# A graph attention block on one core: half of VectorE's evictions listed one step later, behind the score maximum, and the output projection's blocks and sums in another order

## The chip, the cores and the metric

The kernel runs on one core of one Trainium2 chip. The metric is the device time of one execution in microseconds (us). A core has five engines that each work through a list of their own, in the order in which the program gives it: TensorE (PE; its weight loads are PEld in the profile), VectorE (DVE), ScalarE (ACT), GpSimd (POOL), and SyncE (SP), which here issues most of the DMAs. Engines wait for each other at semaphores.

## The reference

The input x has 384 rows (nodes) of 1024 features. With h = relu(layernorm(x)), the block computes

```
q  = h @ wq.T + bq      k  = h @ wk.T + bk      v  = h @ wv.T + bv
q2 = q @ wiq.T + biq    k2 = k @ wik.T + bik    v2 = v @ wiv.T + biv     (16 heads of 64)
scores = q2 @ k2.T / 8 + mask        (per head, 384 x 384; the mask is built from 6528 edges)
out    = x + softmax(scores) @ v2 @ wo.T + bo
```

All seven weights are 1024x1024 in float32.

## The kernel before

**Precision.** Most products are made of three matmuls in a rounded float32: every operand is split into a "hi" part and a "lo" part (lo = value - hi), and the helper `mm3` (lines 373 to 376) issues hi*hi, hi*lo and lo*hi. So whatever leaves PSUM and is multiplied again is evicted twice: ScalarE writes hi, then VectorE (sometimes GpSimd) subtracts and writes lo. The same holds for each 128x1024 slice of a weight: `load` brings it into `raw` over SP's queue (4 buffers), `split_hi` rounds it on ScalarE (L81) or VectorE (L79), `split_lo` writes the rest on VectorE or GpSimd (L86).

**Stages.** First layernorm; then the projections v, q, iv and k with the mask built beside them (up to some 145 us); then a stage in which three things run woven together: the second projections of q and k for eight pairs of heads (generator `fill_qk`), the attention of 48 tiles (16 heads times 3 row tiles), and, when `fill_qk` has run out, the output projection (generator `fill_o`). This last stage is where the change lies.

**The steps of the last stage.** The loop `for i in range(S + 11)` with S = 48 writes the order of all engines' lists by hand; one turn of it is called a step here. `manual_schedule` keeps that order. A step lists, in this order: half of its share of generator work on PE (`fill(r / 2)`), the two score matmuls of tile i (`do_S`, L711), the other half of the share; then `do_ttr(i - 1)` (L717 on VectorE: it reads the scores from PSUM, adds the mask and takes the row's maximum; called ttr below), `do_low` (L748, VectorE), `do_exp(i - 2)` (ScalarE), `do_norm(i - 3)` (L734 and L736 on VectorE, L738 on GpSimd), `do_high` (L744, ScalarE); then PE's transposes of two earlier tiles woven with the product of another head with v2 (`turns_and_av`, L758 and L773); then the evictions of what was transposed one step ago (`do_pt`: hi on ScalarE in L766, lo on VectorE in L767) and of the product of one step ago (`do_ao`: ScalarE L793, VectorE L794), the splitting of a finished pair of heads (`do_aos`: ScalarE L798, GpSimd L799), and the tasks that the generators left (`run_tasks`: `qk_done`, which evicts a finished q or k projection in L384 and L385 and copies it into stacks over SP's queue, and `qk_head`, which splits the weight slice w + 2 and loads the slice w + 5). One tile in three is transposed by a DMA (`do_turn`, L752 on SP) in place of PE. In the steps of `WSTEPS` a slice of wo is prepared by `wo_prep` (split, and the load of the slice three further on).

**The output projection.** The result is six blocks (three row tiles times two halves of 512 columns); block a is `OT[a]`. Each sums eight slices of wo, one per pair of heads: `omm(t, h, k)` adds slice k with one `mm3`. The first four slices (k < KH = 4) make a first half that `ysum` (L663, VectorE) adds into the residual; the other four start a new sum in PSUM. The PSUM banks called "g" are three, and also serve the q and k projections. So a fourth block can start only when the `ysum` of the first has read its bank. `ysums` holds the blocks whose first half is complete; `flush_y(n)` lists the sums of the first n of them. Before, `fill_o` itself calls it, at the moment when a new block asks for its bank:

```
            if k == 0:
                flush_y(1)
                oacc[OT[a]] = bank("g")
            omm(*OT[a], k)
            if k == KH - 1:
                ysums.append(a)
```

**PSUM.** Scores have two banks ("s"), transposes two ("t"), the product with v2 one ("a"), all others three ("g"). From step 49 on, when the scores are done, two of the output's blocks take "s" banks (`bank_step`).

Of the kernel before, what the change touches and what calls it, by code (L numbers as in the profile page):

```python
# [13 lines left out]
PSC = 32768.0  # L14
AF = mybir.ActivationFunctionType
OP = mybir.AluOpType
AX = mybir.AxisListType

N, D, NT, KT, NP = 384, 1024, 3, 8, 8
# [7 lines left out]
def gnn_kernel(ctx: ExitStack, tc: tile.TileContext, x, edges, erows, etw, wq, wk, wv, wiq, wik, wiv, wo,  # L27
# [6 lines left out]
    nc = tc.nc  # L34
# [13 lines left out]
    def bank(tag):  # L48
        return psum.tile([128, 512], F32, tag=tag, name=tag, bufs={"g": 3, "a": 1}.get(tag, 2))

    def gtile(tag):
        return big.tile([128, 2, KT, N], F32R, tag=tag, name=tag)
# [11 lines left out]
    def load(w):  # L64
        if w >= NCH:
            return
        n, m = chunks[w]
        raw[w] = wpool.tile([128, D], F32, tag="raw", name="raw", bufs=4)
        nc.sync.dma_start(raw[w], W[n][m])

    def split_hi(w, dst=None, dve=False):
        if w >= NCH:
            return
        if dst is None:
            t = wpool.tile([128, 2, D], F32R, tag="whl", name="whl", bufs=4)
            dst = (t[:, 0, :], t[:, 1, :])
        whl[w] = dst
        if dve:
            nc.vector.tensor_copy(dst[0], raw[w])  # L79
        else:  # L80
            nc.scalar.activation(dst[0], raw[w], AF.Copy)  # L81

    def split_lo(w, eng=None):
        if w < NCH:
            hi, lo = whl[w]
            (eng or nc.vector).tensor_tensor(lo, raw[w], hi.bitcast(F32), OP.subtract)  # L86

    def split(w, lo_eng=None, dst=None, hi_dve=False):
        split_hi(w, dst, hi_dve)
        split_lo(w, lo_eng)  # L90
# [151 lines left out]
    def mask_select(g):  # L242

        nc.vector.copy_predicated(ma, mbt[g].bitcast(I32), mbt[g])
# [148 lines left out]
    w = 0  # L393
# [109 lines left out]
    top, up, down = vsc[:, 0:1], vsc[:, 1:2], vsc[:, 2:3]  # L503
    accs = [bank("ststag"[i]) for i in range(6)]
    for k in range(8):
        slot_head(w)
        hi, lo = whl[w]
# [82 lines left out]
                    (q2 if r else nc.sync).dma_start(kf[r * 64:(r + 1) * 64, o, :, :], nf[o * 64:(o + 1) * 64, :, :])  # L590
            stacks["k", p] = ks

    tasks = []

    def run_tasks():
        while tasks:
            tasks.pop(0)()

    def qk_head(w):
        if pendq:  # L600
            pendq.pop(0)()
        if 0 < w - W0 < NTAB:
            mask_select(w - W0)
        split_hi(w + 2)
        split_lo(w + 2, nc.gpsimd if (w + 2) % 2 == PAR else None)
        load(w + 5)
        if w == W0:
            mask_select(0)
# [19 lines left out]
    WO = NCH - 8  # L628

    DT = (0,)  # L630
    PRE, RATE, RATE_O, RATE_E = 84, 7.9, 8, 8
    WSTEPS = (37, 40, 42, 44, 47, 51)
    PAR, OPOOL, ODVE = 1, (2, 3, 4, 6), (2,)

    otile = {}
# [1 line left out]
    KH = 4  # L637

    def wo_prep(k):

        dst = None
        if k == 4:
            otile[0] = gtile("g3").rearrange("p a k n -> p (a k n)")
        if 4 <= k < 7:
            g, b = otile[0], (k - 4) * 2048
            dst = (g[:, b:b + 1024], g[:, b + 1024:b + 2048])
        split(WO + k, nc.gpsimd if k in OPOOL else None, dst, k in ODVE)
        load(WO + k + 3)

    def omm(t, h, k, c=(0, 512)):  # L650
        hi, lo = (a[:, h * 512 + c[0]:h * 512 + c[1]] for a in whl[WO + k])
        mm3(oacc[t, h][:, c[0]:c[1]], ao[:, 0, k, t * 128:(t + 1) * 128], ao[:, 1, k, t * 128:(t + 1) * 128],
            hi, lo, k in (0, KH), k in (KH - 1, KT - 1))
# [3 lines left out]
    now = [-1]  # L657
    wready = [0, 0] + [99] * 6

    def ysum(a, c=(0, 512)):  # L660
        t, h = OT[a]
        y = xb[t][:, h * 512 + c[0]:h * 512 + c[1]]
        nc.vector.tensor_tensor(y, oacc[t, h][:, c[0]:c[1]], y, OP.add)  # L663
        return y
# [3 lines left out]
    def flush_y(n=6):  # L668
        for _ in range(min(n, len(ysums))):
            ysum(ysums.pop(0))  # L670

    def fill_o():


        first = [(0, 0), (0, 1), (1, 0), (1, 1), (2, 0), (2, 1)]
        first += [(a, k) for k in (2, 3) for a in range(3)] + [(a, k) for a in range(3, 6) for k in range(KH)]
        for a, k in first:
            while now[0] < wready[k] or now[0] < 6 * k + OREADY:
                yield 0
            if k == 0:  # L680
                flush_y(1)
                oacc[OT[a]] = bank("g")
            omm(*OT[a], k)
            if k == KH - 1:
                ysums.append(a)
            yield 4
        bank_step = (0, 0, 0, 49, 50)
        todo = [(a, k) for k in range(KH, 7) for a in range(5)]
        while todo:
            ready = [q for q in todo if now[0] >= max(6 * q[1] + OREADY, wready[q[1]], bank_step[q[0]])]  # L690
            if not ready:
                yield 0
                continue
            a, k = ready[0]
            todo.remove(ready[0])
            if k == KH:
                flush_y(1)
                oacc[OT[a]] = bank("gggss"[a])
            omm(*OT[a], k)
            yield 4  # L700

    st_ps, es, sts, tps, avs, aof = {}, {}, {}, {}, {}, {}
    S = 48

    def do_S(i):
        h, t = divmod(i, 3)
        p, o = divmod(h, 2)
        qs, ks = stacks["q", p], stacks["k", p]
        ps = st_ps[i] = bank("s")
        for s in range(2):  # L710
            nc.tensor.matmul(ps[:, :N], qs[:, o, t * 128:(t + 1) * 128], ks[:, o, s, :], start=(s == 0), stop=(s == 1))  # L711

    def do_ttr(i):
        t = i % 3
        e = es[i] = work.tile([128, N], F32, tag="e", name="e", bufs=EB)
        s = sts[i] = work.tile([128, 4], F32, tag="s", name="s", bufs=12)
        nc.vector.tensor_tensor_reduce(e, st_ps.pop(i)[:, :N], ma[:, t, :], -0.125, 3.0e38, OP.add, OP.min, s[:, 0:1])  # L717
# [43 lines left out]
    def do_pt(i):  # L761
        h, t = divmod(i, 3)
        pt = ptv[h % 3]
        hi, lo = (pt[:, s * 3:s * 3 + 3, t * 128:(t + 1) * 128] for s in range(2))
        pv = tps.pop(i)[:, :N].rearrange("p (k n) -> p k n", k=3)
        nc.scalar.activation(hi, pv, AF.Copy, scale=PSC)  # L766
        nc.vector.scalar_tensor_tensor(lo, pv, PSC, hi, op0=OP.mult, op1=OP.subtract)  # L767

    def av_mm(h):
        ps = avs[h] = bank("a")  # L770
# [15 lines left out]
    def do_ao(h):  # L786
        p, o = divmod(h, 2)
        if o == 0:
            aof[p] = work.tile([128, N], F32, tag="aof", name="aof")
        tmp = work.tile([128, N], F32, tag="aot", name="aot", bufs=1)  # L790
        ps = avs.pop(h)
        m, l = slice(o * 64, o * 64 + 64), slice(64 - o * 64, 128 - o * 64)
        nc.scalar.activation(tmp[m, :], ps[l, :N], AF.Identity, scale=down[l], bias=bc[m, 40 + p:41 + p])  # L793
        nc.vector.scalar_tensor_tensor(aof[p][m, :], ps[m, :N], down[m], tmp[m, :], op0=OP.mult, op1=OP.add)  # L794

    def do_aos(h):
        p = h // 2
        nc.scalar.activation(ao[:, 0, p, :], aof[p], AF.Copy)  # L798
        nc.gpsimd.tensor_tensor(ao[:, 1, p, :], aof[p], ao[:, 0, p, :].bitcast(F32), OP.subtract)  # L799
# [4 lines left out]
    def fill(n):  # L804
        credit[0] += n
        while credit[0] > 0 and gens:
            try:
                c = next(gens[0])
            except StopIteration:
                gens.pop(0)  # L810
                continue
            if c == 0:
                credit[0] = 0.0
                return
            credit[0] -= c
# [4 lines left out]
    t_at, a_at = {}, {}  # L820
    for h in range(16):
        for t in (1, 2):
            t_at.setdefault(3 * h + 7 if h < 15 else 3 * h + 5 + t, []).append(3 * h + t)
        a_at[3 * h + 10 if h < 15 else 3 * h + 9] = h
    for i in range(S + 11):
        now[0] = i
        r = RATE if len(gens) == 2 else RATE_O if i < S else RATE_E
        fill(r / 2)
        if i < S:
            do_S(i)  # L830
        fill(r / 2)
        if 0 <= i - 1 < S:
            do_ttr(i - 1)
        if 0 <= i - 4 < S and (i - 4) % 3 in DT:
            do_low(i - 4)
        if 0 <= i - 2 < S:
            do_exp(i - 2)
        if 0 <= i - 3 < S:
            do_norm(i - 3)
            if (i - 3) % 3 in DT:  # L840
                do_high(i - 3)
        turns_and_av(t_at.get(i, []), [a_at[i]] if i in a_at else [])
        for x in t_at.get(i - 1, []):
            do_pt(x)
        if i - 1 in a_at:
            do_ao(a_at[i - 1])
        if a_at.get(i - 2, 0) % 2:
            do_aos(a_at[i - 2])
        run_tasks()
        if 0 <= i - 4 < S and (i - 4) % 3 in DT:  # L850
            do_turn(i - 4)
        if i in WSTEPS:
            wo_prep(wp)
            wready[wp] = i + 2
            wp += 1
    while gens:
        now[0] = 999
        fill(999)
# [55 lines left out]
```

## Time and profile before

| | |
|---|---|
| median of 3 runs | 296.02 us (294.78, 296.02, 296.08) |
| the profiled execution | 294.56 us, of which the span from first to last instruction is 292.8 us |
| granted TensorE clock | 1.000 over the span |
| PE busy | 284.7 us (97%), 1610 instructions |
| VectorE busy | 208.2 us (71%), 509 instructions |
| ScalarE busy | 159.7 us (55%), 291 instructions |
| GpSimd busy | 154.8 us (53%), 153 instructions |
| VectorE from 160 us to 250 us | between 6.65 and 8.16 us busy in each 10 us |
| VectorE from 260 us to 270 us | 8.41 us busy of 10 |

How to read it: busy time is the time that an engine's instructions occupy it; matmuls are pipelined, so a PE that is busy all the time can still be fed unevenly. "Idle before, releaser" of an instruction is how long its engine stood still before it and which event of another engine ended that. Buffers are named without their numbers: "g" is a PSUM bank of the three or a large SBUF tile of the same name, "whl" a split weight slice, "s" a bank of scores or the small tile of row sums, "res" the residual. Positions in time are us from the span's start.

### The profile page before, as it was taken

The numbers are of one execution on the slowest core, as the hardware profiler recorded it, in microseconds if no ns is written. First come the engines' busy times: TensorE is split into PE (matmuls) and PEld (weight loads), VectorE is DVE, ScalarE is ACT, GpSimd is POOL, SyncE is SP. The second block draws the span as 40 slices with busy tenths as digits, with TensorE's granted clock in tenths as the row PEclk, the third lists the DMA queues.
The fourth block names the chain that finished last, engine by engine and source line by source line (L and its number), as shares of the span: only waits on it lengthen the run. The fifth ranks groups of instructions, "written<-read, shape, count | busy, mean of one in ns | idle before, by whom it ended". The sixth has DMA issues, their size and how long they took to land. (4 is left out here: it accounts for less than half of the span.)

```text
span 292.8 us, 4859 instructions
## 1 busy us (share of the span) xinstructions
PE 284.7 (97%) x1610; PEld 267.4 (91%) x1610; DVE 208.2 (71%) x509; ACT 159.7 (55%) x291; POOL 154.8 (53%) x153
## 2 busy tenths in 40 slices
PE   6999999999999999999999999999999999989995
PEld 5999999999988889999999999999999998868874
DVE  3858996667665452999966768878786876788623
ACT  3894543244331222343643778787878788766510
POOL 3765576437775787992004256262627268636210
PEclk9999999999999999999999999999999999999999
DMA  7799857973463342278438879879797969901105
GB/s 268 248 321 404 292 209 254 323 242 112 143 189 122 121 146 72 72 224 296 154 86 227 241 208 211 212 166 227 166 234 147 254 133 234 230 2 27 27 3 215
DMA packets 33305, 54.60 MB, mean 187 GB/s; under 512 B 17408, under 2 KB 20992, under 8 KB 33280
## 3 DMA queue, kind: packets, MB, share of 16 engines
q1 hardware_dynamic: 30896, 51.90, 61.4%
q0 software_dynamic: 2064, 1.80, 2.2%
q10 hardware_dynamic: 320, 0.59, 0.8%
q8 instruction: 13, 0.21, 0.3%
q14 instruction: 12, 0.10, 0.1%
HBM read 38.30 MB, written 3.39 MB: 142 GB/s over the span
## 5 line engine op out<-in xcount | busy, mean ns | idle before, releaser
L374 PE MATMUL g<-g,whl 128*128 128x384 f32 x312 | 105.8, 339 | 0.0
L376 PE MATMUL g<-g,whl 128*128 128x384 f32 x312 | 104.3, 334 | 0.0
L375 PE MATMUL g<-g,whl 128*128 128x384 f32 x312 | 104.2, 334 | 0.0
L231 POOL DMA_INDIRECT tab<-val,idx x51 | 59.7, 1171 | 32.0 <-issue 11.8
L81 ACT ACTIVATE whl<-raw 128x1024 fp32r<-128x1024 f32 x51 | 53.5, 1050 | 29.8 <-PE g L376 21.1
L86 DVE TENSOR_TENSOR whl<-raw,whl 128x1024 fp32r<-128x1024 f32 x41 | 53.8, 1313 | 20.1 <-ACT whl L81 17.0
L374 PEld LDWEIGHTS g<-g,whl 128*128 128x128 f32 x312 | 58.6, 188 | 0.2
L375 PEld LDWEIGHTS g<-g,whl 128*128 128x128 f32 x312 | 58.6, 188 | 0.0
L376 PEld LDWEIGHTS g<-g,whl 128*128 128x128 f32 x312 | 58.6, 188 | 0.1
L390 ACT ACTIVATE g<-f,bc 128x384 fp32r<-128x384 f32 x24 | 14.8, 618 | 53.7 <-DVE f L389 44.8
L738 POOL TENSOR_TENSOR e<-e,s 128x384 f32<-128x384 f32 x32 | 26.4, 829 | 31.2 <-DVE s L734 23.0
L86 POOL TENSOR_TENSOR whl<-raw,whl 128x1024 fp32r<-128x1024 f32 x11 | 26.3, 2395 | 25.9 <-ACT whl L81 25.0
L721 ACT ACTIVATE e<-e,s 128x384 f32<-128x384 f32 x48 | 29.1, 607 | 2.0 <-DVE s L717 1.2
L717 DVE CUSTOM_DVE_ANT_0 e<-s,ma 128x384 f32<-128x384 f32 x48 | 26.4, 552 | 4.3 <-PE s L711 3.7
L389 DVE TENSOR_TENSOR f<-g,rrow 128x384 f32<-128x384 f32 x24 | 13.3, 554 | 18.0 <-PE g L376 18.0
L773 PE MATMUL a<-pt,vhl 128*128 128x384 f16 x96 | 26.1, 326 | 0.0
L758 PE MATMUL t<-ident,e 128*128 128x128 f32 x96 | 24.9, 272 | 0.0
L711 PE MATMUL s<-ks,qs 128*128 128x384 f32 x96 | 24.5, 335 | 0.0
L767 DVE SCALAR_TENSOR_TENSOR pt<-t,pt 128x384 f16<-128x384 f32 x32 | 16.6, 549 | 8.2 <-ACT pt L766 8.2
L799 POOL TENSOR_TENSOR g<-aof,g 128x384 fp32r<-128x384 f32 x8 | 8.3, 1041 | 25.5 <-ACT g L798 25.5
L711 PEld LDWEIGHTS s<-ks,qs 128*128 128x128 f32 x96 | 17.5, 188 | 0.9
L744 ACT ACTIVATE pt<-e,s 128x384 f16<-128x384 f32 x16 | 9.9, 616 | 15.4 <-issue 9.4
(166 smaller groups left out, 447.0 us busy)
## 6 DMA issues: line engine op xcount, KB each, us to landing
ks<-nat SPq DMA_DIRECT2D x30, 192.0 KB
raw<-in_wv_dram SPq DMA_DIRECT2D x8, 512.0 KB
raw<-in_wq_dram SPq DMA_DIRECT2D x8, 512.0 KB
raw<-in_wiv_dram SPq DMA_DIRECT2D x8, 512.0 KB
raw<-in_wk_dram SPq DMA_DIRECT2D x8, 512.0 KB
raw<-in_wiq_dram SPq DMA_DIRECT2D x8, 512.0 KB
raw<-in_wik_dram SPq DMA_DIRECT2D x8, 512.0 KB
raw<-in_wo_dram SPq DMA_DIRECT2D x8, 512.0 KB
```

What stands on the lines that cost most here:

```text
L81: nc.scalar.activation(dst[0], raw[w], AF.Copy)
L86: (eng or nc.vector).tensor_tensor(lo, raw[w], hi.bitcast(F32), OP.subtract)
L231: nc.gpsimd.indirect_dma_start(out=tabs[c // RNG], out_offset=bass.IndirectOffsetOnAxis(ap=idx[:, c:c + 1], axis=0), in_=val[:, c:c + 1], ...
L374: nc.tensor.matmul(ps, lhi, rhi, start=first, stop=False)
L375: nc.tensor.matmul(ps, lhi, rlo, start=False, stop=False)
L376: nc.tensor.matmul(ps, llo, rhi, start=False, stop=last)
L711: nc.tensor.matmul(ps[:, :N], qs[:, o, t * 128:(t + 1) * 128], ks[:, o, s, :], start=(s == 0), stop=(s == 1))
L717: nc.vector.tensor_tensor_reduce(e, st_ps.pop(i)[:, :N], ma[:, t, :], -0.125, 3.0e38, OP.add, OP.min, s[:, 0:1])
L721: nc.scalar.activation(es[i], es[i], AF.Exp, bias=s[:, 0:1], scale=-1.0, accum_out=s[:, 1:2])
L738: nc.gpsimd.tensor_tensor(es[i], es[i], s[:, 2:3].to_broadcast([128, N]), OP.mult)
L758: nc.tensor.transpose(ps[:, k * 128:(k + 1) * 128], es[i][:, k * 128:(k + 1) * 128], ident)
L773: nc.tensor.matmul(ps[:, :N], vhl[:, k, h, :, :], ptv[h % 3][:, 3 * s + k, :], start=(k == 0 and s == 0), stop=(k == 2 and s == 1))
```

## The change

Four things are changed in the last stage.

1. A list `later` is added, and `run_later()`, called in each step just behind `do_ttr`. Four kinds of VectorE instructions are put there in place of being listed at once, so that they stand one step later, behind the next step's ttr: the lo of a weight slice (`split_lo` in `qk_head` and `wo_prep`, where VectorE does it), the lo of transposed tiles (`do_pt`), and the second half of `do_ao`. `do_aos`, which reads the result of `do_ao`, moves from step i - 2 to i - 3 of its head, and the loop has one step more.
2. `fill_o` no longer calls `flush_y`; `flush_y()` stands at the end of every step, and lists the sums of all blocks completed by then.
3. The order of the output's `mm3`: the first three blocks now go by pairs of slices (block 0 with slices 0 and 1, block 1, block 2, then each with 2 and 3), where before slice 2 went over the three blocks and then slice 3. In the second half block 2, which takes a "g" bank, comes behind blocks 3 and 4.
4. `WSTEPS` begins with 36 and 38 in place of 37 and 40, so that slices 2 and 3 of wo are prepared one and two steps sooner, with the loads that these calls issue.

```diff
-    tasks = []
+    tasks, later = [], []
+
+    def run_later():
+        for f in later[:]:
+            f()
+        later.clear()
...
         split_hi(w + 2)
-        split_lo(w + 2, nc.gpsimd if (w + 2) % 2 == PAR else None)
+        eng = nc.gpsimd if (w + 2) % 2 == PAR else None
+        if eng is None and now[0] >= 0:
+            later.append(lambda: split_lo(w + 2))
+        else:
+            split_lo(w + 2, eng)
         load(w + 5)
...
-    WSTEPS = (37, 40, 42, 44, 47, 51)
+    WSTEPS = (36, 38, 42, 44, 47, 51)
     PAR, OPOOL, ODVE = 1, (2, 3, 4, 6), (2,)
...
-        split(WO + k, nc.gpsimd if k in OPOOL else None, dst, k in ODVE)
+        split_hi(WO + k, dst, k in ODVE)
+        if k in OPOOL:
+            split_lo(WO + k, nc.gpsimd)
+        else:
+            later.append(lambda: split_lo(WO + k))
         load(WO + k + 3)
...
-        first = [(0, 0), (0, 1), (1, 0), (1, 1), (2, 0), (2, 1)]
-        first += [(a, k) for k in (2, 3) for a in range(3)] + [(a, k) for a in range(3, 6) for k in range(KH)]
+        first = [(a, k) for c in (0, 2) for a in range(3) for k in (c, c + 1)]
+        first += [(a, k) for a in range(3, 6) for k in range(KH)]
...
             if k == 0:
-                flush_y(1)
                 oacc[OT[a]] = bank("g")
...
-        todo = [(a, k) for k in range(KH, 7) for a in range(5)]
+        todo = [(a, k) for k in range(KH, 7) for a in (0, 1, 3, 4, 2)]
...
             if k == KH:
-                flush_y(1)
                 oacc[OT[a]] = bank("gggss"[a])
...
-        nc.vector.scalar_tensor_tensor(lo, pv, PSC, hi, op0=OP.mult, op1=OP.subtract)
+        later.append(lambda: nc.vector.scalar_tensor_tensor(lo, pv, PSC, hi, op0=OP.mult, op1=OP.subtract))
...
-        nc.vector.scalar_tensor_tensor(aof[p][m, :], ps[m, :N], down[m], tmp[m, :], op0=OP.mult, op1=OP.add)
+        dst = aof[p][m, :]
+        later.append(lambda: nc.vector.scalar_tensor_tensor(dst, ps[m, :N], down[m], tmp[m, :], op0=OP.mult, op1=OP.add))
...
-    for i in range(S + 11):
+    for i in range(S + 12):
...
             do_ttr(i - 1)
+        run_later()
...
-        if a_at.get(i - 2, 0) % 2:
-            do_aos(a_at[i - 2])
+        if a_at.get(i - 3, 0) % 2:
+            do_aos(a_at[i - 3])
...
             wp += 1
+        flush_y()
     while gens:
```

## The prediction

> **What bounds the kernel now.** I read the page first.
>
> ```profile
> PE 284.7 (97%) x1610; PEld 267.4 (91%) x1610; DVE 208.2 (71%) x509; ACT 159.7 (55%) x291; POOL 154.8 (53%) x153
> ...
> PEclk9999999999999999999999999999999999999999
> ```
>
> TensorE is busy for 284.7 of 292.8 us at full clock, so at most 8.1 us can be won by feeding it better, and the change adds and removes no matmul. The second view is who PE waits for, over the whole span:
>
> ```profile
> PE s L295 <- ACT g L283: 1.5, 1, 1.5
> PE g L315 <- POOL ident masks.py:199: 1.4, 1, 1.4
> PE g L374 <- DVE res L663: 1.4, 1, 1.4
> PE g L295 <- DVE g L287: 0.4, 1, 0.4
> ```
>
> Three of the four lie in the first 10 us, which the diff does not touch. The third is the only wait in the last stage: a block of the output projection asks for its bank and the `ysum` of an earlier block (L663) has not read it yet. The rest of the 8.1 us is the start and the 3.3 us between the last matmul and the last output byte. The third view is the timeline at that place, VectorE and then PE:
>
> ```profile
> 256.49 0.56 DVE L767 SCALAR_TENSOR_TENSOR pt<-t,pt 128x384 f16<-128x384 f32 x1 [0.26 <-ACT pt L766]
> 257.18 0.62 DVE L794 SCALAR_TENSOR_TENSOR aof<-a,vsc,aot 64x384 f32<-64x384 f32 x1
> 258.27 1.23 DVE L86 TENSOR_TENSOR g<-raw,g 128x1024 fp32r<-128x1024 f32 x1 [0.46 <-ACT g L81]
> 259.51 0.69 DVE L663 TENSOR_TENSOR res<-g,res 128x512 f32<-128x512 f32 x1
> ```
>
> ```profile
> 258.37 0.51 PE L711 MATMUL s<-ks,qs 128*128 128x384 f32 x2
> 260.25 0.50 PE L374 MATMUL g<-whl,g 128*128 128x512 f32 x1 [1.37 <-DVE res L663]
> 260.59 0.40 PE L375 MATMUL g<-whl,g 128*128 128x512 f32 x1
> ```
>
> Block 1 had its last matmul of slice 3 at 252.3, but its sum was listed only when block 4 asked for the bank, behind the evictions of step 44 and the 1.23 us lo of a wo slice, which itself waits for ScalarE. So it ran 7 us later, and PE stood.
>
> **The change part by part.** The sum is made against the profiled execution (294.56 us: span 292.8 and 1.76 around it).
>
> *The sum of a block at the end of its step.* The pair L711 occupies 0.35 us of PE's order (256.62 to 256.98, one cycle earlier), so L374 would have started at 258.72; it started at 260.25: 1.53 us. It took 0.34 to the next start where its neighbours take 0.23: another 0.11. Together 1.64 us on PE, which is the path. In the new order the built lists place sum 0 before ttr(41), sum 1 before ttr(42), sum 2 before ttr(43) (ttr(n): the maximum of tile n). PE completes those blocks at about 249.8, 251.6 and 253.3. Walking VectorE's new list by the durations above (ttr 0.55, L767 0.5, L794 0.61, L748 0.62, sum 0.62 to 0.69) the sums end near 250.5, 253.6 and 255.6; blocks 3, 4 and 5 ask at 253.6, 258.7 and 263.9. The 1.64 us go, with 3 us or more to spare.
>
> *What waits instead.* A sum now stands in front of a ttr and waits for PE's last matmul of the step; behind it queue ttr, two L767, L794, the reciprocals, and through them ScalarE's exponentials and GpSimd's products. By the same walk: sum 0 cannot start before 249.8, so L767 and L794 of step 40 end at 252.7 (before: 250.9) and the transposes and the head product that need their banks start at 254.3: 1.6 to spare. ttr(45) ends at 262.1; score pair 47 reuses its bank at 263.5: 1.4 to spare. The sum of block 5 ends at about 270.1; block 2, now behind blocks 3 and 4, asks at 271.1: 1.0. The last L794 before head 15 ends at 276.6 against 277.6: 1.0. So nothing new ends up on PE: 0; the bounds are nothing below, and above what the rivals give.
>
> *`later`, before the output stage.* Per three steps (6.84 us of PE) VectorE has some 5.3 us of work. At 213.9 the ttr stood behind L385 and L86 and ran at 215.05, 2.4 us after its scores were there (212.66); now it runs at once, and L86 after it, ending at 215.3 instead of 215.1. L767 and L794 end 0.8 to 1 us later (224.7 for 223.9) and PE needs their banks at 226.7 and 226.8: 2 us. The weight's lo is needed two slices, some 13 us, later. PE has no wait here now, so an earlier ttr earns nothing: 0. If the cover were gone, each step of delay beyond 2 us would cost its excess once per head.
>
> *`do_aos` a step later.* Its L799 lands at least two steps before the matching slice is multiplied, except for the last pair, where the engines have nothing else listed: in the trace L799 ends at 283.28 and costs PE 0.11 at 283.33, and the chain (L793, L794, L798, L799) still starts from the same matmul. 0.
>
> *Slices 2 and 3 sooner.* VectorE's cast L79 (0.69) moves before ttr(36), which then ends at 239.9 instead of 239.2; score pair 38 needs it at 242.9. GpSimd's L86 for slice 3 (2.37) ends at 247.0, first use at 248.9 (before: 250.4 and 250.8). The load of slice 5 is listed on SP before the four `ks` copies of the last pair; it waits for GpSimd's lo of slice 1 (done at 237.8) and for the DMA transpose at 239.68, so it leaves at about 240.9 and the copies some tenths later than 241.35. They feed score pair 42 at 251.5. 0, with a bound in the rivals.
>
> *VectorE beside GpSimd.* These rows do not agree with a fixed duration:
>
> ```profile
> 266.82 2.40 POOL L86 TENSOR_TENSOR g<-raw,g 128x1024 fp32r<-128x1024 f32 x1 [2.08 <-ACT g L81]
> ...
> 267.88 1.75 DVE L748 SCALAR_TENSOR_TENSOR pt<-e,s,pt 128x384 f16<-128x384 f32 x1 [0.24 <-ACT pt L744]
> ```
>
> L748 takes 0.62 at its median; beside GpSimd's L86 it took 1.75, ending 0.4 after it. VectorE's L86 shows the same in the mask stage (2.15 and 2.43 at 117.3 and 121.6, otherwise 1.23). The change puts GpSimd's slice 2 (from 239.3) beside L748 of tile 33 (239.9): held to 241.8 or so, then L385 and ttr(37) by 243.4, and score pair 39 asks at 244.65. Still 1.2 to spare, so I take 0.
>
> The Trainium skill, SBUF — State Buffer, section "Who interferes with whom", says that a VectorE instruction with two SBUF inputs and a GpSimd instruction that reads SBUF exclude each other, the later one waiting for the whole of the other. The 1.75 us agree with it. By that rule the sum stays at -1.64 as long as the holds fall where the walk puts them, and the first rival is what it gives if they fall one step worse.
>
> Sum: -1.64. Profiled execution 294.56 to 292.9; median 296.02 to 294.4. The runs shown spread by 1.30 us, and the profiled one lies 1.46 below their median; I predict from the median.
>
> **The rivals.** *VectorE falls behind GpSimd in steps 42 to 45.* In the walk L748 of tile 39 starts at 254.2 and GpSimd's lo of slice 4 at 254.65. If ScalarE or VectorE is 0.5 us later than I have it, L748 comes second and is held up to 2.38; VectorE's L86 of slice 5, at 259.4, can in the same way meet GpSimd's two L738 (1.61 together). That makes 4.0 us in one queue; ttr(45) had 1.4, so score pair 47 waits 2.6, less the 1.64 won: 297.0. It decides from 1.4 us of delay, and is slower than now from 3.0. For it: VectorE is busy 8.41 of 10 us after 260. Against: such a hold was seen once in sixteen L748, and each has its margin.
>
> *The `ks` copies land late.* Half a MB ahead of them at the page's 230 GB/s is 2.3 us, VectorE's hold adds 1.2: 3.5 late at most. The trace gives no landing time; they were issued by 244.2 and needed at 251.5. If they had no slack now it gives 294.4 + 3.5 = 297.9. Against: no score pair waited for its copies.
>
> *The stall comes back at another block.* Block 2's second half has 1.0 us of cover and the bank is the same kind. If sum 5 comes 2.6 late, 1.64 is paid again: 296.0.
>
> **How the numbers follow.** Forecast 0.62, VectorE behind GpSimd 0.16, `ks` copies 0.07, stall elsewhere 0.15. Half a per cent, about what a measurement of this kernel can tell from no change, is 1.48 us, and 1.64 lies just beyond it. Of the forecast's 0.62 I give 0.45 to faster and 0.17 to within (a stall that is smaller in the executions measured). The stall elsewhere is within, as is 0.03 of the first rival; the other 0.13 and the copies are slower. Faster 0.45, same 0.35, slower 0.20. The range goes from 292.9 (the profiled execution less the stall) to 297.0 (the first rival); the forecast alone is 292.9 to 295.0.
>
> **What would show it.** In the changed profile PE's waits should hold no `res` L663, L374 after the score pair 45 should start 0.35 after it, L663 should run near 250, 253 and 255, and the last matmul should start near 287.5 instead of 289.2. L748 of tile 33 should take more than 1 us. I am wrong if PE shows a new wait on L717 (score bank), L767 or L794 (banks "t" and "a"), or on a DMA at score pair 42, or if the start and the tail move by more than 0.3 us.

## The result, and the profile after

The changed kernel takes 292.91 us (median of 6 runs, 292.77 to 293.17); the kernel before 294.81 us (6 runs, the three of the table above among them, 294.34 to 296.08). The ratio is 0.9934 with a 95% interval of 0.9914 to 0.9955: faster by 0.66%, 1.90 us, where the forecast was 294.4 us. The profiled executions are 294.56 and 292.88 us, 1.68 us apart; the spans 292.8 and 291.2.

The line of busy times in the profile after:

```profile
PE 285.0 (98%) x1610; PEld 267.7 (92%) x1610; DVE 207.6 (71%) x509; ACT 159.5 (55%) x291; POOL 153.0 (53%) x153
```

Same work, a shorter span. The chain of PE's waits after (engine, buffer, line, whom it waited for, total us, times, longest):

```profile
PE g L315 <- POOL ident masks.py:199: 1.4, 1, 1.4
PE g L295 <- DVE g L287: 0.7, 1, 0.7
PE s L295 <- ACT g L283: 0.7, 1, 0.7
```

The wait of `omm` (L374) on `ysum` is gone and nothing has come in the last stage; the three left lie in the first 10 us. The timelines after, of PE at the old place and of VectorE's `ysum` (L676 here) and `do_low` (L759):

```profile
258.42 0.51 PE L722 MATMUL s<-ks,qs 128*128 128x384 f32 x2
258.77 0.39 PE L374 MATMUL g<-whl,g 128*128 128x512 f32 x1
...
287.56 0.28 PE L376 MATMUL t<-whl,g 128*128 128x256 f32 x1
```

```profile
239.69 2.54 DVE L759 SCALAR_TENSOR_TENSOR pt<-e,s,pt 128x384 f16<-128x384 f32 x1
...
250.00 0.69 DVE L676 TENSOR_TENSOR res<-g,res 128x512 f32<-128x512 f32 x1 [1.72 <-PE g L376]
...
252.79 0.68 DVE L676 TENSOR_TENSOR res<-g,res 128x512 f32<-128x512 f32 x1
...
253.86 0.62 DVE L759 SCALAR_TENSOR_TENSOR pt<-e,s,pt 128x384 f16<-128x384 f32 x1
...
254.47 0.67 DVE L676 TENSOR_TENSOR res<-g,res 128x512 f32<-128x512 f32 x1
```

L374 starts 0.35 us behind the score pair 45, where it started 1.88 behind it. The sums run at 250.0, 252.8 and 254.5, none of them at the moment when a bank is asked for. The last matmul starts at 287.56 instead of 289.17: 1.61 us sooner, and the 3.6 us behind it are unchanged. So the time comes from the place that the prediction named, and in the size that it worked out. What has to be explained is why the forecast of 294.4 is nevertheless 1.5 us too high.

### The profile page after: what moved, and what is told of

It reads as the page before. It is cut to its first block, busy times and chain, and to the rows that moved or that the text cites. A ratio compares the mean times of both kernels' runs of the same rounds, so it can differ in the third digit from the quotient of the medians.

```text
span 291.2 us, 4856 instructions
## 1 busy us (share of the span) xinstructions
PE 285.0 (98%) x1610; PEld 267.7 (92%) x1610; DVE 207.6 (71%) x509; ACT 159.5 (55%) x291; POOL 153.0 (53%) x153
## 4 chain that ended last, share of the span: by engine, by line
PE 95%; DMA 2%; DVE 1%; SPq 0%; issue 0%
PE g L376 22%; PE g L375 22%; PE g L374 22%; PE s L722 6%; PE a L784 5%; PE t L769 4%; DMA g<-in_x_dram 2%; PE s L376 2%; PE s L374 2%; PE s L375 2%; PE g L423 2%; PE t L376 2%; PE t L375 2%; PE t L374 2%; PE a L376 1%; PE a L375 1%
## 5 line engine op out<-in xcount | busy, mean ns | idle before, releaser
L374 PE MATMUL g<-g,whl 128*128 128x384 f32 x312 | 105.8, 339 | 0.0
L231 POOL DMA_INDIRECT tab<-val,idx x51 | 58.4, 1145 | 33.7 <-DMA tab<-val,idx 10.0
L86 DVE TENSOR_TENSOR whl<-raw,whl 128x1024 fp32r<-128x1024 f32 x41 | 53.6, 1307 | 16.3 <-ACT whl L81 16.3
L374 PEld LDWEIGHTS g<-g,whl 128*128 128x128 f32 x312 | 58.6, 188 | 0.2
L86 POOL TENSOR_TENSOR whl<-raw,whl 128x1024 fp32r<-128x1024 f32 x11 | 26.4, 2396 | 25.0 <-ACT whl L81 23.7
L391 DVE SCALAR_TENSOR_TENSOR g<-f,bc,g 128x384 fp32r<-128x384 f32 x24 | 16.7, 699 | 0.7 <-ACT g L390 0.7
```

The source lines that it names most:

```text
L231: nc.gpsimd.indirect_dma_start(out=tabs[c // RNG], out_offset=bass.IndirectOffsetOnAxis(ap=idx[:, c:c + 1], axis=0), in_=val[:, c:c + 1], ...
L374: nc.tensor.matmul(ps, lhi, rhi, start=first, stop=False)
```

## The experiments

The theory: the stall at L374 is the whole gain, and no edit wins it by itself, since where one removes the stall something else takes its place. Two rivals: edit 2 (the sums at the end of a step) does it alone and the rest is idle; or the earlier ttr of edit 1 does. Besides that it was asked how much cover VectorE has left, and where a level of 296 us comes from.

**Each edit alone.** e1_flush is the kernel before with edit 2 only, e2_later with edit 1 only, e3_order with edits 3 and 4 only.

```diff
 # e1_flush, against before
-                flush_y(1)
                 oacc[OT[a]] = bank("g")
...
+        flush_y()          # at the end of each step
 # e3_order, against before
-    WSTEPS = (37, 40, 42, 44, 47, 51)
+    WSTEPS = (36, 38, 42, 44, 47, 51)
...
-        first = [(0, 0), (0, 1), (1, 0), (1, 1), (2, 0), (2, 1)]
-        first += [(a, k) for k in (2, 3) for a in range(3)] + [(a, k) for a in range(3, 6) for k in range(KH)]
+        first = [(a, k) for c in (0, 2) for a in range(3) for k in (c, c + 1)]
+        first += [(a, k) for a in range(3, 6) for k in range(KH)]
...
-        todo = [(a, k) for k in range(KH, 7) for a in range(5)]
+        todo = [(a, k) for k in range(KH, 7) for a in (0, 1, 3, 4, 2)]
```

> The kernel before, with edit 2 alone (the sums listed at the end of the step in which their block is complete). Theory A (the 1.64 us are the place of block 1's sum in VectorE's list, and whatever takes it out from behind the evictions of step 44 wins all of it): no PE wait on L663, L374 after the score pair 45 starts 0.35 after it, profile about 292.9 us, 1.6 us under the kernel before. Rival B (only the sum's own listing matters): the same here. Rival C (it takes the evictions moved back as well, since the sum alone then queues behind them at another place): a wait of 0.5 to 1.6 us remains on L663.

Measured: 293.76 us median (10 runs), ratio 0.9963 (0.994 to 0.9986). The `ysum` wait is gone, but PE has a new one, at score pair 46. VectorE and GpSimd in this kernel (L746 is `do_low`, L715 the ttr), and PE:

```profile
253.84 2.35 DVE L746 SCALAR_TENSOR_TENSOR pt<-e,s,pt 128x384 f16<-128x384 f32 x1
...
259.01 1.23 DVE L86 TENSOR_TENSOR g<-raw,g 128x1024 fp32r<-128x1024 f32 x1
260.27 0.56 DVE L715 CUSTOM_DVE_ANT_0 e<-s,ma 128x384 f32<-128x384 f32 x1
```

```profile
253.40 2.38 POOL L86 TENSOR_TENSOR g<-raw,g 128x1024 fp32r<-128x1024 f32 x1 [2.21 <-ACT g L81]
```

```profile
260.89 0.62 PE L709 MATMUL s<-ks,qs 128*128 128x384 f32 x2 [0.61 <-DVE s L715]
```

This is the prediction's first rival, met in a part of the change and one step earlier (score pair 46, not 47): `do_low` of tile 39 comes 0.44 us behind GpSimd's lo of slice 4 and is held for all of it (2.35 instead of 0.62), the lo of slice 5 still stands ahead of the ttr, and the score bank is 0.78 late. In the whole change the same `do_low` starts at 253.86, before GpSimd's L86 (254.60), and takes 0.62. So edit 2 alone gives half of the gain, and is not the whole change.

> Edit 1 alone (the four kinds of VectorE instructions behind the next ttr, the split of head pairs a step later); the sums are still listed when a new block asks for its bank, the block order and WSTEPS are those of before. Its list has sum 1 ahead of ttr 44, with the lo of the wo slice behind it. Theory A: the wait at 258.7 goes here too, 1.4 to 1.6 us under the kernel before; sum 0 ends by the durations at 253.5 for a block that asks at 253.6, so up to 0.2 us may stay there. Rival B: the sum waits as before, 1.6 us on L663, time as before. Rival C: half of it remains.

Measured: 294.5 us median (10 runs), ratio 0.9976 (0.9954 to 0.9997), but that is no gain: its ten executions all lie at 294.3 to 294.7, where two thirds of those of the kernel before lie too (294.4 to 294.9), and the others of that kernel are on the upper level treated below. The old stall is gone: the sum of block 1 now stands ahead of ttr(44), and is done in time without edit 2. In its place two others appear among PE's waits:

```profile
PE g L375 <- POOL whl L86: 0.7, 1, 0.7
PE g L374 <- DVE res L676: 0.2, 1, 0.2
```

Slice 3 of wo is multiplied at 252.05 where 251.23 was its turn, since GpSimd's lo of it ran from 249.60. The second wait is that of block 0, whose second half takes the bank of block 3 (the sum waited for is the fourth of the six, and the last matmul of block 5 starts only at 267.48, behind it). VectorE, then PE:

```profile
267.33 0.68 DVE L676 TENSOR_TENSOR res<-g,res 128x512 f32<-128x512 f32 x1
```

```profile
268.07 0.50 PE L374 MATMUL g<-g,g 128*128 128x512 f32 x1 [0.20 <-DVE res L676]
```

The sum of block 3 is listed only when block 0 asks for the bank, and so PE starts 0.36 us late. The next two experiments show which edits take these waits away: edit 2 the wait on the sum, edits 3 and 4 together the wait on slice 3. So edit 1 alone removes the old stall, as theory A said, but wins no time, as it did not say.

> Edits 3 and 4 alone (order of the output's blocks, slices 2 and 3 prepared sooner). Block 1's sum is still listed at block 4's request, behind the evictions of step 44 and the lo of the wo slice. Theories A, B and C: the wait of 1.6 us on L663 stays and the time is that of before. The rival that the block order itself wins the time (block 1 is complete 1.7 us earlier): the wait falls by 0.7 us or more. L748 of tile 33 is held beside GpSimd's slice 2: over 2 us instead of 0.62, without a wait of PE.

Measured: 294.75 us median (10 runs), ratio 0.9984 (0.9959 to 1.0009), no difference. The old wait stands as it was:

```profile
PE g L374 <- DVE res L663: 1.4, 1, 1.4
```

**Two of three.** e5_later_flush has edits 1 and 2 without 3 and 4; e6_later_order is the changed kernel without edit 2.

> Edits 1 and 2 together, without 3 and 4. e1_flush and e2_later each lost the wait at 258.7 and met another (0.78 us on a score bank; 0.92 us on GpSimd's lo of slice 3 and 0.47 us on the sum of block 5). Theory now: the first comes from VectorE's evictions standing ahead of the ttr and goes with edit 1; the second is slice 3 prepared too late and needs edit 4. So here PE waits some 0.9 us for GpSimd's L86 at 251 and for nothing else in the last stage: about 293.9 us on the level of 294.56. Rival (edits 3 and 4 change nothing, as e3_order alone seemed to say): no wait, 292.9.

Measured: 294.07 us median (10 runs, of which four lie at 295.3 to 295.8 and six at 293.6 to 294.1), ratio 0.9981 (0.9955 to 1.0006). One wait is left in the last stage, slice 3's lo:

```profile
PE g L375 <- POOL whl L86: 0.7, 1, 0.7
```

The theory was right: slice 3 starts 0.83 us late, and the six lie some 0.9 us above the changed kernel. The wait on a sum is gone though edit 3 is missing, so it is edit 2 that removes it. The hold of `do_low` of tile 39 is here too (2.44 us, begun 0.36 us behind GpSimd's L86) and no score pair waits: with edit 1 the ttr no longer stands behind the lo of slice 5. No run has edit 3 without edit 4 or the other way round, so what each of these two is worth alone stays open.

> The changed kernel with edit 2 undone: the sums are listed at the request of a new block again, edits 1, 3 and 4 stay. Theory now: edit 1 already takes sum 1 out from behind the lo of the wo slice, edit 4 readies slice 3, and block 2 behind 3 and 4 gives sum 5 its time: no PE wait in the last stage, the time of the changed kernel, 292.9. Rival (the sum's own listing, edit 2, is what wins): the wait of 1.6 us on L663 is back and the time 294.5.

Measured: 293.63 us median (10 runs, four at 295.1 to 295.2, six at 293.2 to 293.7), ratio 0.9974 (0.9951 to 0.9997). The wait is again that of block 0 on the sum of block 3, which is listed only when asked for: 0.36 us, with the slower starts around it 0.57. The expectations of this run and of the one before took it for the sum of block 5, and so for the work of edit 3; but edit 3 is in this kernel and the wait is still there. The result lies between the theories: edit 2 is worth only these last 0.4 us once the others are there, though alone it was worth 0.8 (294.5 to 293.7). The edits are no sum of four gains. Edits 1 and 2 each remove the old stall, each uncovers a smaller one behind it, and it takes the others to cover these.

**GpSimd's hold of tile 33.** e4_lo2 is the changed kernel with slice 2's lo on VectorE.

```diff
-    PAR, OPOOL, ODVE = 1, (2, 3, 4, 6), (2,)
+    PAR, OPOOL, ODVE = 1, (3, 4, 6), (2,)
```

> The changed kernel with the lo of wo slice 2 on VectorE in place of GpSimd. If VectorE's 2.54 us for L759 of tile 33 is the hold beside GpSimd's L86 at 239.43, it falls to 0.62 here, and only tile 45 keeps 1.2 to 1.8 us. VectorE gets 1.23 us more in step 37. By the theory that VectorE's holds have cover in this kernel the time stays within 0.2 us of the changed kernel; by the rival that the cover is thin, it changes by 0.5 us or more.

Measured: 292.86 us median (6 runs), ratio 0.9944 (0.9906 to 0.9981). VectorE's timeline at that place:

```profile
239.62 1.22 DVE L86 TENSOR_TENSOR whl<-raw,whl 128x1024 fp32r<-128x1024 f32 x1
240.76 0.61 DVE L759 SCALAR_TENSOR_TENSOR pt<-e,s,pt 128x384 f16<-128x384 f32 x1
```

The 2.54 us of `do_low` are 0.61 again, so it was GpSimd's L86 that held it, and the time does not move: the hold was covered, as the walk had it.

**How much cover there is.** e7_delay1 and e8_delay3 are the changed kernel with one and three more instructions on VectorE in step 45, behind `run_later` and so ahead of ttr(45); their result is used nowhere.

```diff
+        if i == 45:
+            for _ in range(1):        # e8_delay3: range(3)
+                nc.vector.tensor_reduce(vmax[:, 7:8], ma.rearrange("p t n -> p (t n)"), axis=AX.X, op=OP.max)
```

> The changed kernel with one maximum over the 1152 elements of the mask (some 1.34 us by L526's 0.68 for 512) added to VectorE's list in step 45, behind the lo of the wo slice; its result is not used. It measures the cover: ttr 45 ends at 262.12, PE takes some 0.14 to see it, and score pair 47 starts at 263.52, so 1.26 us are free. Theory (cover as measured): a wait of 0.1 us, time within 0.2 us of the changed kernel. Rival (each us of VectorE in this stretch is on the path): 1.3 us more.

Measured: 293.06 us median (10 runs), ratio 0.9954 (0.9929 to 0.9979); the profiled execution 292.99 against 292.88. No wait, only 0.08 us more in score pair 47 (0.44 us to the next start for 0.36). The 1.4 us of cover that the prediction gave this pair are there, and 1.3 us use them up.

> The same with three such maxima, 4.0 us. Theory: score pair 47 waits 4.0 - 1.26 = 2.75 us for its ttr, and all else moves with it: 2.75 us more than the changed kernel, 295.6 us. If it is much less, VectorE's list has more slack than the walk says; if it is 4.0, it has none.

Measured: 297.42 us median (4 runs), ratio 1.0087 (1.0055 to 1.012), 297.28 in the profiled execution: 4.40 us above the changed kernel's. The wait is as long as expected. But what follows it is not; PE's timeline, and under it busy time and granted clock by stretch of the trace (stretch, its length, PE busy, instructions, granted clock, DMA share, GB/s):

```profile
263.27 0.40 PE L376 MATMUL g<-whl,g 128*128 128x512 f32 x1
266.27 0.62 PE L722 MATMUL s<-ks,qs 128*128 128x384 f32 x2 [2.60 <-DVE s L728]
...
268.40 0.63 PE L374 MATMUL g<-whl,g 128*128 128x512 f32 x1
268.82 0.63 PE L375 MATMUL g<-whl,g 128*128 128x512 f32 x1
```

```profile
266.00:268.00 2.00, 1.73 (x8) 0.95 0.00 0
268.00:270.00 2.00, 2.00 (x6) 0.50 0.50 98
270.00:271.00 1.00, 1.00 (x4) 0.50 0.00 0
271.00:272.00 1.00, 1.00 (x6) 0.90 0.00 0
272.00:274.00 2.00, 2.00 (x15) 1.00 0.00 1
```

TensorE idled for 2.60 us, and 1.4 us after it had work again its clock was halved for 3.4 us: matmuls start 0.43 us apart instead of 0.23. From 267.66 to 271.30 nine of them take 3.64 us where nine times 0.23 is 2.07: 1.57 lost. With 2.77 for the wait and 0.11 for the restart that makes 4.45, and 4.40 was measured.

**Where 296 us comes from.** The kernel before took 295.99 to 296.30 us in 26 of its 81 executions in all comparisons, and near 294.5 in most others; most other versions show such a second level, 1.4 to 2.0 us above their first. Two profiled executions (of e5_later_flush and e6_later_order) fell on the upper level. The start of PE's timeline, after, and then in e6_later_order:

```profile
6.65 0.66 PE L295 MATMUL s<-ident,g 128*128 128x128 f32 x4 [0.70 <-ACT g L283]
...
7.58 0.88 PE L315 MATMUL g<-ident 128*128 128x128 f32 x6
...
10.88 2.27 PE L423 MATMUL g<-g,whl 128*128 128x256 f32 x17
```

```profile
6.60 1.12 PE L295 MATMUL s<-ident,g 128*128 128x128 f32 x4 [0.64 <-ACT g L283]
...
8.36 1.49 PE L315 MATMUL g<-ident 128*128 128x128 f32 x6
...
12.48 0.50 PE L423 MATMUL g<-g,whl 128*128 128x256 f32 x2 [0.33 <-ACT whl L351]
```

The same transposes go at half pace, and the first projection (L423) starts at 12.48 instead of 10.88: 1.6 us, about the difference of the levels, lost before the first weight is used. The clock column shows 1.00 in both, so that at the start of a trace the spacing tells more than the column. Three kernels test it, with another number of warm-up transposes (L315) ahead: e9_warm24 the changed kernel with 24, e10_before24 the kernel before with 24, e11_warm12 the changed one with 12.

```diff
-    WARM = (20, 6, 0)
+    WARM = (24, 6, 0)          # e11_warm12: (12, 6, 0)
```

> The changed kernel with 24 instead of 20 warm-up transposes at the start, so that TensorE stays busy up to the first transposes of the input (20 end at 5.96 us at the slow pace of 0.23 us each, those begin at 6.6; 24 end near 6.8). Theory: the upper of the two levels of every version (some 1.65 us higher, a quarter to a third of the executions) is TensorE going at half pace until about 10.4 us, because its idle time of 0.6 us before 6.6 us spoils the busy stretch after which the clock is raised; with that gap filled the pace rises by about 8.2 us at the latest, so that no execution lies 1.4 us or more above the lowest, and the median is 292.8 to 293.3. Rival (the level comes from something else, such as the order in which the first transfers land): a quarter to a third of the executions stay near 294.5.

Measured: 292.93 us median (292.84 to 293.21, 6 runs), ratio 0.9934 (0.991 to 0.9959).

> The kernel before with 24 instead of 20 warm-up transposes. Theory: no execution at 296.0 to 296.3, all between 294.3 and 295.2, median near 294.6; the difference to e9_warm24 is then that of the change alone, 1.6 us (1.5 to 1.8). Rival: 296.0 to 296.3 in a quarter to a third of the executions.

Measured: 294.50 us median (294.34 to 294.77, 12 runs), ratio 0.9979 (0.9961 to 0.9996). None of these 18 executions is on the upper level, while 9 of 23 of the kernel before were in the same comparison. In both profiles the pace rises before the 24 transposes have ended (they take 4.52 and 4.63 us, where 20 at half pace take 4.53), and the idle time in front of the first real ones is still there (0.68 and 0.62 us). The changed kernel has 0.70 us of it too, and no loss. So it is shown that the longer warm-up removes the level; that it does so by filling this gap when the pace rises late is argued. The change alone, with the level out of the way, is 294.50 - 292.93 = 1.57 us.

> The changed kernel with 12 warm-up transposes: they end near 4.2 us and TensorE is idle for some 2.4 us before the first transposes of the input. Theory: in most executions or all the pace is still half from 6.6 us on, for 3 us or more, and the median lies at 294.5 or above. Rival: the warm-up has nothing to do with the two levels; the median stays at 292.9 with a quarter to a third of the executions at 294.5.

Measured: 294.51 us median (293.8 to 295.18, 12 runs), ratio 0.9982 (0.9961 to 1.0003): no longer two levels but a spread, all of it above the changed kernel's 292.9. The median is just where the theory had its lower end, and no execution is untouched, though six of twelve lost less than it expected. The lowest, which is the profiled one (293.8), by stretch:

```profile
7.00:8.00 1.00, 1.00 (x12) 1.00 0.95 363
8.00:9.00 1.00, 1.00 (x7) 0.51 1.06 411
9.00:10.00 1.00, 1.00 (x7) 0.50 0.74 258
10.00:11.00 1.00, 0.94 (x5) 0.50 0.28 73
11.00:12.00 1.00, 1.00 (x9) 0.78 0.51 68
```

Here the column does record it: an idle time of 2.47 us (to 6.73), then full pace for 1.3 us, then half clock for 3.4 us, as in e8_delay3. So this execution was not at half pace from 6.6 us on, as the theory had it, but fell to it at 8.0; L423 starts at 11.85, 0.97 later than in the changed kernel, and the execution is 0.92 longer. The rival, that the warm-up has nothing to do with the levels, is out. What no profile shows is an execution of e9_warm24 or e10_before24 in which the clock rises late; for these the times alone speak.

## Why the prediction was wrong in its number and right in its steps

**The step that failed** is the last line of the sum: "Profiled execution 294.56 to 292.9; median 296.02 to 294.4 ... I predict from the median". The prediction had seen that the three runs spread by 1.30 us and that the profiled one lay 1.46 below their median, and read this as scatter. It was two levels: by their times, two of the three runs (296.02 and 296.08) had the slow start that 26 of 81 have, the third and the profile had not. From the profiled execution the same sum gives 292.9, and 292.91 was measured. None of the six runs of the changed kernel fell on the upper level, two of the six of the kernel before did. That is a part of the 1.90 us between the medians; the 55 executions of the kernel before that are not on the upper level have a median of 294.53, 1.62 us above the changed kernel.

By the Trainium skill, TensorE: Matmul & The Clock Gate, Part 1, "What's actually happening", the clock is decided by a window of 3.4 us that runs freely and does not start with the kernel, so that the time at which it rises differs from run to run. The two levels, and the 3.4 us at half clock in e8_delay3 and e11_warm12, agree with it. The same section of the Trainium skill also says that the clock falls after an idle window of about 3.4 us. Here 2.47 and 2.60 us of idle time were enough, while the 1.37 us of the old stall and the 0.61 us of e1_flush left it at full.

**The stall.** 1.64 us predicted. 1.68 between the profiled executions, 1.57 in the pair with 24 warm-up transposes. Right.

**The walk of the sums.** The prediction had them end near 250.5, 253.6 and 255.6; they end at 250.7, 253.5 and 255.1. ttr(45) was to end at 262.1 and ends at 262.12, with score pair 47 at 263.52. The sum of block 5 was to end at 270.1 against 271.1 and ends at 269.4 against 271.03. Right, and e7_delay1 shows that the 1.4 us of cover are real.

**What moves cost nothing.** `later`, `do_aos` and the earlier slices: no wait anywhere, right. But the prediction costed the earlier slices as a move that earns nothing and costs nothing. e2_later and e5_later_flush show what edits 3 and 4 do: without them the lo of slice 3 is 0.83 us late. The zero was right for the whole change, and it hid that these edits keep the 1.64 us from being paid back in part. For block 2 behind 3 and 4, the second half of edit 3, no run shows a wait that it removes: in e5_later_flush, without it, block 2 starts its second half 0.18 us after the sum of block 5 has ended, in the changed kernel 1.63 us after it.

**VectorE beside GpSimd.** Held "to 241.8 or so" and ttr(37) done by 243.4: held to 242.2, done by 243.21, and e4_lo2 shows that it was covered. Right. Its **first rival** did not come in the whole change and did come in e1_flush, with one hold of 2.35 us instead of two. Its price was too low: in e8_delay3 an idle time of 2.60 us on PE costs 4.4, so that from its base of 296.02 this rival stood for 296.02 - 1.64 + 4.4 = 298.8 and not 297.0 us. That its 297.0 lies near the 297.42 of e8_delay3 is luck: a price 1.8 too low and a base 1.46 too high. The other two rivals did not occur in the changed kernel; a late sum at another block did come in e2_later and e6_later_order, but at block 0, and the `ks` copies were not tried by themselves.

**The chances.** Faster had 0.45, and 0.17 of the forecast's share went to "within" because 1.64 lies just beyond half a per cent. With the level known the doubt would have been the same: 1.64 us of 294.56 are 0.56%, and the interval of the measured ratio reaches to 0.9955, a gain of less than half a per cent.

## What to carry to other kernels

Look at the single times before you choose the one to predict from: when a profiled execution lies well below the median, find out first whether the times come in two groups, and predict from the group that the profile belongs to. A stall on a buffer that is released by an instruction in another engine's list is worth its whole length only if the next buffers in that list have cover as well; take the edits apart, and the waits that each leaves behind show which ones carry the rest. And keep TensorE's idle stretches short, at the start too: here 1.4 us did the clock no harm, and 2.5 us was paid for a second time.

## What the runs showed of the hardware that was not expected

An idle time of TensorE of 2.47 or 2.60 us is followed, 1.3 to 1.4 us after the work resumes, by 3.4 us at a granted clock of 0.50; in the output projection this cost 1.57 us on top of the stall. At the start of a program the clock comes up at a moment that differs between executions, and with 20 warm-up transposes 1.6 to 1.7 us hang on that; with 24 they did not in 18 executions. And `do_low`, a VectorE instruction with two inputs in SBUF, is held by GpSimd's L86 for nearly all of it when it starts 0.26 to 0.44 us behind it (2.54, 2.44 and 2.35 us), and for nothing when it starts 0.74 us ahead (0.62).
